# Projections of an attention layer taken two tiles at a time, as seven block products in place of eight

## The chip, the cores and the metric

The kernel runs on one core of a Trainium2 chip. The metric is the device time of one launch in microseconds (us). The kernel before took 3641.48 us, the median of three runs (3638.69 to 3645.62).

The core has five engines with instruction streams of their own: TensorE (PE in the profile, with its weight loads as PEld), VectorE (DVE), ScalarE (ACT), GpSimd (POOL) and SyncE (SP), which here only issues transfers. Each takes its instructions in order and waits on semaphores for the others.

## The reference, cut to what matters

The input x has 64 sequences of 32 tokens of width 512, float32 throughout. Four layers are added to x one after the other. Layer 0 is a linear layer per sequence with a feed-forward part and a normalisation. Layer 1 is a gated feed-forward layer with low-rank updates per sequence. Layer 2 is paged attention, followed by a linear layer with low-rank experts. Layer 3 mixes the tokens of each sequence and applies another linear layer. The change is in layer 2's attention, and in what layer 1 prepares for it:

```python
q = jnp.einsum('bsd,ed->bse', x, Wq).reshape(bsz, seqlen, HQ, D)   # HQ 32, D 128
k = jnp.einsum('bsd,ed->bse', x, Wk).reshape(bsz, seqlen, HK, D)   # HK 8
v = jnp.einsum('bsd,ed->bse', x, Wv).reshape(bsz, seqlen, HK, D)
q = _rope(_rmsnorm(q, q_norm_w), pos)
k = _rope(_rmsnorm(k, k_norm_w), pos)
...                                # 512 cached keys and values per sequence, then the own 32
probs = jax.nn.softmax(scores, axis=-1)
o = jnp.einsum('bhqk,bkhd->bqhd', probs, v_all)
return jnp.einsum('bse,de->bsd', o, Wo)
```

## The kernel before

The 2048 tokens are 16 tiles of 128 tokens, that is of four sequences. The kernel has one stage per layer; in time, layer 0 ends near 390 us, layer 1 near 1059, attention near 3477, and the tail (the rest of layer 2, and layer 3) takes the remainder. The order of the work on TensorE is the order in which the program emits it, since every matmul goes through `c.on_pe` (L74), which chains it to the one before.

**Layer 1** (loop from L512) works through eight groups of two tiles. TensorE computes the gate and up features, `new.features(0)` to `features(10)`. Between those calls stand the calls that load the next group's x and low-rank matrices, and `sum_up` (L272): for each of 16 blocks of Wo, SP loads a row of blocks (`rows`), GpSimd makes four differences of them (`add`, 128x256 each, L289 to L292) and SP stores them to a DRAM buffer `wo_sums` (`store`).

**Attention** is done in two halves, each with four of the eight key heads and half of the query heads, and within a half tile by tile: 32 steps, each with a half h and a tile T. A step has 16 turns, one per sequence and key head, and a turn has two slots, so that two steps, a pair, have 64 slots. Per turn i TensorE transposes the probabilities of turn i (L684), does what is planned for the turn's first slot, takes the scores of turn i+2 (L900), does what is planned for its second slot, and multiplies the values of turn i (L689). The chain of a softmax is scores in PSUM (one buffer), VectorE's multiply by scale with mask and minimum (L905), ScalarE's exponential (L907), VectorE's reciprocal (L909) and product (L912), transposes and ScalarE's copy (L918). At the start of every slot, `slot` (L1044) pops up to two entries of the list `later`: a quarter of the next sequence's key loads (16 transfers of 64 KB make a block of a sequence, from SP) or a load of a piece of Wo (`next_wo`). Cached values are gathered by GpSimd (L715).

The **projections** of a step (class `Projection`, L751) are planned into the slots of the step before, by the tables `plan` (products) and `then` (transposes), L1063 to L1094. For v, k and four groups of query heads, `product` makes an output of 128x512 from four chunks of x, two in each of two slots, into one of two PSUM buffers of the tag "mm" (L786), which the output products also use. A v output is copied by ScalarE. For k and q, `rotated` (L735) runs at once: ScalarE squares the output (L728), VectorE sums the squares (L730), VectorE and GpSimd make the inverse root (L731, L128), VectorE multiplies by cosine and, in two halves, by sine, all read from PSUM (L741, L744), and GpSimd adds the two and multiplies by the root (L747, L748). `turned` (L797) then transposes the result on TensorE. The prologue ahead of the first slot projects the first tile this way. All projection weights of a half, six of 1 MB (`weights`, L953), stay in SBUF; they are loaded at the start and once more at the change of halves.

The **output** of a pair (class `Outputs`, L828) is done in the following pair, by the slots in `ats` (L1109). It is already one of seven block products: the two tiles' output makes a 2x2 block matrix, and so do the weights, some of them the sums made in layer 1. Pieces of Wo of 512 KB come through four buffers; a product that has used one appends `next_wo`. Two tiles `y` are stored by SP at slot 70, that is slot 6 of the pair after. In the last pair the same places hold `tail.weights` and `tail.fold`, which prepare the tail's weights.

## Time and profile before

| | |
|---|---|
| median of three runs | 3641.48 us |
| profiled execution, its own time | 3648.7 us |
| its span, first to last instruction | 3646.9 us |
| TensorE clock granted, mean | 0.998 |
| TensorE busy | 3589.7 us, 19520 instructions |
| VectorE busy | 1894.8 us |
| ScalarE busy | 1296.2 us |
| GpSimd busy | 1415.8 us |
| DMA | 527 MB, mean 145 GB/s |
| attention prologue | 1059 to 1087.5 us |
| first pair, steady pairs | 136.1 us, 149 to 152 us each |

The profile is one execution. A group line reads: source line, engine, operation, output from inputs by the program's names, shapes, count; then busy us and mean ns of one; then the engine's idle time just before them and what ended most of it. A float32 matmul is two instructions on TensorE. Matmuls overlap, so that a sum of their durations is more than the time they take from TensorE. In a window, numbers stand for busy time per engine.

### The profile page before, as it was taken

What the parts mean: (1) busy time and instruction counts of PE and PEld (TensorE: products, weight loads), DVE (VectorE), ACT (ScalarE), POOL (GpSimd) and SP (SyncE); (2) the same over time, 40 slices, a digit from 0 to 9 for tenths busy, and PEclk for the clock granted to TensorE, in tenths of its full rate; (3) what the DMA queues carried; (4) which work ended last, traced back from release to release, by engine and by line L of the source; (5) the groups of instructions that cost most, each with busy time, mean ns of one, the idle gap of its engine ahead of it and who ended that gap; (6) DMA issues with size and microseconds to landing.
All of it is one profiled execution on the core that took longest, in us unless ns stands there. A gap on an engine that the chain in (4) does not pass through costs nothing.

```text
span 3646.9 us, 60352 instructions
## 1 busy us (share of the span) xinstructions
PE 3589.7 (98%) x19520; PEld 2665.6 (73%) x19520; DVE 1894.8 (52%) x4932; ACT 1296.2 (36%) x3046; POOL 1415.8 (39%) x1407
## 2 busy tenths in 40 slices
PE   8999999999999999999999999999999999999999
PEld 3444788888866777777777877778777788777855
DVE  5453222222236655666666656566666666666533
ACT  1111111111115544444444444444444444444311
POOL 0112430000025544555445454454555544545232
PEclk9999999999999999999999999999999999999999
DMA  5004541111124566555555565555555555556631
GB/s 211 24 27 170 171 152 55 50 45 36 38 93 133 149 186 185 155 171 153 185 183 153 181 219 179 179 151 182 174 181 169 156 186 178 170 175 201 218 97 62
DMA packets 527914, 527.15 MB, mean 145 GB/s; under 512 B 54162, under 2 KB 441234, under 8 KB 527602
## 3 DMA queue, kind: packets, MB, share of 16 engines
q1 hardware_dynamic: 480882, 371.21, 32.9%
q0 software_dynamic: 44416, 147.88, 12.6%
q10 hardware_dynamic: 2304, 4.20, 0.3%
q8 instruction: 159, 2.61, 0.3%
q14 instruction: 153, 1.25, 0.1%
HBM read 493.72 MB, written 29.36 MB: 143 GB/s over the span
## 4 chain that ended last, share of the span: by engine, by line
PE 85%; DVE 8%; ACT 2%; DMA 2%; issue 1%; SPq 1%; DVEq 0%; POOL 0%; another core or an unknown queue 0%; ACTq 0%; POOLq 0%
PE po L689 12%; PE sc L900 11%; PE gate_up L342 10%; PE pq L689 9%; PE py L689 9%; PE prT_ps L684 5%; PE pz L342 5%; PE po L1249 3%; PE ph L124 3%; PE pk L689 3%; PE pv L689 3%; PE pd L249 2%; DVE own_vt L722 2%; PE po L342 2%; DVE pr L905 1%; PE qkT_ps L684 1%
## 5 line engine op out<-in xcount | busy, mean ns | idle before, releaser
L715 POOL DMA_INDIRECT vt<-in_v_rows,v_rows x512 | 499.9, 976 | 594.6 <-PE po L689 484.2
L907 ACT ACTIVATE pr<-pr,low 128x544 f32<-128x544 f32 x512 | 383.5, 749 | 703.5 <-DVE low L905 630.4
L689 PEld LDWEIGHTS po<-prT,vt 128*128 128x128 f32 x4096 | 531.3, 192 | 111.1 <-issue 80.7
L900 PE MATMUL sc<-kt,qT 128*128 128x288 f32 (+1 forms) x2048 | 556.3, 394 | 5.5 <-ACT qT L803 1.7
L689 PE MATMUL po<-prT,vt 128*128 128x128 f32 x4096 | 543.9, 276 | 9.5 <-ACT prT L918 6.3
L905 DVE CUSTOM_DVE_ANT_0 pr<-sc,mask 128x544 f32<-128x544 f32 x512 | 368.8, 720 | 321.8 <-PE sc L900 288.5
L900 PEld LDWEIGHTS sc<-kt,qT 128*128 128x128 f32 x2048 | 370.6, 190 | 156.0 <-issue 62.0
L689 PE MATMUL pq<-wq,xT 128*128 128x512 f32 x1024 | 480.6, 592 | 0.0
L918 ACT COPY prT<-prT_ps 128x512 f32<-128x512 f32 x512 | 295.3, 577 | 202.1 <-PE prT_ps L684 147.6
L912 DVE TENSOR_SCALAR pr<-pr,low 128x512 f32<-128x512 f32 x512 | 341.1, 666 | 15.1
L684 PE MATMUL prT_ps<-ident,pr 128*128 128x128 f32 x2048 | 311.2, 275 | 0.1
L689 PEld LDWEIGHTS pq<-wq,xT 128*128 128x128 f32 x1024 | 185.8, 190 | 132.4 <-issue 125.3
L909 DVE RECIPROCAL low<-low 128x1 f32<-128x1 f32 x512 | 83.5, 163 | 340.8 <-ACT pr L907 305.7
L684 PEld LDWEIGHTS prT_ps<-ident,pr 128*128 128x128 f32 x2048 | 238.1, 142 | 7.9 <-issue 0.3
L689 PE MATMUL py<-wo,oT 128*128 128x256 f32 x1024 | 241.4, 379 | 0.0
L128 POOL TENSOR_TENSOR rs<-rs,minus_half 128x4 f32<-128x4 f32 x160 | 169.2, 1058 | 162.9 <-DVE rs L731 158.1
L910 ACT ACTIVATE own_pr<-pr,low 128x32 f32<-128x32 f32 x512 | 164.0, 320 | 131.0 <-DVE low L909 120.3
L747 POOL TENSOR_TENSOR rot<-rot,swapped 128x512 f32<-128x512 f32 x160 | 205.0, 1281 | 5.1 <-DVE swapped L744 3.9
L689 PEld LDWEIGHTS py<-wo,oT 128*128 128x128 f32 x1024 | 187.6, 190 | 21.9
L722 DVE COPY own_vt<-v 32x128 f32<-32x128 f32 x512 | 173.1, 338 | 38.3 <-PE po L689 13.9
L689 PE MATMUL py<-wo,o_sum 128*128 128x256 f32 x768 | 181.3, 379 | 2.1 <-DMA wo<-wo_sums 1.3
L426 DVE TENSOR_TENSOR sg<-sg,gate_up 128x256 f32<-128x256 f32 (+1 forms) x88 | 37.0, 421 | 276.0 <-ACT sg L425 276.0
(226 smaller groups left out, 5192.9 us busy)
## 6 DMA issues: line engine op xcount, KB each, us to landing
kt<-in_kT SPq DMA_DIRECT2D x2048, 64.0 KB
wo<-wo_sums SPq DMA_DIRECT2D x128, 512.0 KB
wo<-in_WoT SPq DMA_DIRECT2D x96, 512.0 KB
xt<-x SPq DMA_DIRECT2D x48, 256.0 KB
A<-in_A SPq DMA_DIRECT2D x64, 152.0 KB
...
```

The costliest lines, as they stand in the source:

```text
L128: self.nc.gpsimd.tensor_tensor(t, t, self.minus_half[:, :n], ALU.pow)
L342: c.on_pe(nc.tensor.matmul(out, lhsT, rhs, start=start, stop=stop))
L684: c.on_pe(nc.tensor.transpose(pt[:, m, :], piece, c.ident))
L689: c.on_pe(nc.tensor.matmul(out, lhsT, rhs, start=first and i == 0, stop=last and i == len(pairs) - 1))
L715: nc.gpsimd.indirect_dma_start(out=vts[b % 2][:, n, :], out_offset=None, in_=a["v_rows"], in_offset=bass.IndirectOffsetOnAxis(ap=rows[h][: ...
L722: nc.vector.tensor_copy(own_vts[b % 2][g * S:(g + 1) * S, g % 2, :], v[j * S:(j + 1) * S, g * HD:(g + 1) * HD])
L747: nc.gpsimd.tensor_tensor(r, r, tmp, ALU.add)
L900: c.on_pe(nc.tensor.matmul(sc[:, lo + n * PSIZE:lo + m * PSIZE].rearrange("p (n k) -> p n k", k=PSIZE), q, kt[:, n:m, g, :], start=True, s ...
L905: nc.vector.tensor_tensor_reduce(pr[:, :NK], sc[:, lo:lo + NK], masks[h, b], -SCALE, 3.0e38, ALU.add, ALU.min, low[:, 0:1])
L907: nc.scalar.activation(pr[:, :NK], pr[:, :NK], AF.Exp, bias=low[:, 0:1], scale=-1.0, accum_out=low[:, 1:2])
L912: nc.vector.tensor_scalar(pr[:, :L], pr[:, :L], low[:, 2:3], None, ALU.mult)
L918: nc.scalar.copy(prT, pt)
```

## The change

The projections of the two tiles of a pair are made together. For each of three groups (k and v, query groups 0 and 1, query groups 2 and 3) x is a 2x2 block matrix (two tiles by two halves of the 512 inputs) and the weights are another (two halves of the inputs by two outputs of 512 columns). Seven products of blocks are made instead of eight, each over two chunks. Products 1 and 5 are copied out of PSUM by ScalarE; the other five are added by VectorE to a tile in SBUF, and two more additions per group are made from SBUF to SBUF. The sums of x blocks are made by GpSimd (`x_sums`). The rotation reads the finished tile in SBUF, writes in place, and is emitted at the start of the next slot (`soon`, `the_rest`).

The weights come in pieces of 512 KB: plain blocks for products 1, 2 and 3, and sums for 4 to 7. The sums of all weights, 40 block sets in place of 16, are made by GpSimd in layer 1, five per group of tiles, with loads on SP, and stored from GpSimd's own queue. Pieces pass through four buffers "wp" and, for the first pair, also through the four "wo"; every product appends a load (`next_wp`) to `later`. All of a pair's projections stand in the pair before, by one table for both steps; the prologue makes those of the first pair. The output products stand at other slots of the pair, from slot 0 and again from slot 53. The tail's weights use buffers of x, work and weight pools.

```diff
-def sum_up(c, pool, sums, h, k):
...
+def sum_up(c, pool, blocks, dst):
+    nc = c.nc
+    w = []
     def rows():
+        w.append(pool.tile([P, 4, D // 2], F32, name="blocks", bufs=2))
+        for n, block in enumerate(blocks):
+            c.load_by(w[0][:, n, :], block)
     def add():
+        t = pool.tile([P, 4, D // 2], F32, name="sums")
+        (b11, b12, b21, b22), (t1, t2, t3, t4) = ([v[:, n, :] for n in range(4)] for v in (w[0], t))
         nc.gpsimd.tensor_tensor(t1, b12, b11, ALU.subtract)
         nc.gpsimd.tensor_tensor(t3, b22, b12, ALU.subtract)
         nc.gpsimd.tensor_tensor(t2, b22, t1, ALU.subtract)
         nc.gpsimd.tensor_tensor(t4, b21, t2, ALU.subtract)
+        nc.gpsimd.dma_start(dst, t)
+    return rows, add
+def column_blocks(a, h, g):
+    if g == 0:
+        return [a[n][:, h * D:(h + 1) * D] for n in ("WkT", "WvT")]
+    at = (h * HKP + 2 * (g - 1)) * D
+    return [a["WqT"][:, at + n * D:at + (n + 1) * D] for n in range(2)]
+def all_sums(c, pool, sums):
+    a, H = c.a, D // 2
+    for h in range(HALVES):
+        for g in range(GB):
+            left, right = column_blocks(a, h, g)
+            for k in range(KC // 2):
+                for n in range(2):
+                    q = slice(n * H, (n + 1) * H)
+                    yield sum_up(c, pool, [w[(k + KC // 2 * i) * P:(k + KC // 2 * i + 1) * P, q]
+                                           for i in range(2) for w in (left, right)],
+                                 sums["in", h][:, g, :, k, q])
+        for k in range(HQP // 2):
+            rows = [(h * HQP + n * HQP // 2 + k) * HD for n in range(2)]
+            yield sum_up(c, pool, [a["WoT"][at:at + HD, n * H:(n + 1) * H] for at in rows for n in range(2)],
+                         sums["out", h][:, k])
...
             def load_x(self):
-                self.xs = [c.load(xp, "xt", [P, D], x_in(G * self.g + t)) for t in range(G)]
+                self.xs = [xp.tile([P, D], F32, name="xt") for _ in range(G)]
+                for t in range(G):
+                    c.load_by(self.xs[t], x_in(G * self.g + t))
...
+            parts = [f for _ in range(5) for f in next(to_sum)]
+            def features(f):
+                new.features(f)
+                if f < len(parts):
+                    parts[f]()
...
+        def the_rest():
+            for f in soon:
+                f()
+            del soon[:]
         def squares_and_root(src):
             tmp = wk.tile([P, REP, HD], F32, name="squares")
             nc.scalar.activation(tmp, src, AF.Square)
-            rs = qp.tile([P, REP], F32, name="rs")
+            rs = qp.tile([P, REP], F32, name="rs", bufs=4)
...
-        def rotated(psrc, tab):
...
+        def rotated(t, tab):
+            src = t.rearrange("p (h d) -> p h d", d=HD)
             ct, st = tab
             rs = squares_and_root(src)
+            tmp = wk.tile([P, REP, HD], F32, name="swapped", bufs=2)
             for lo, hi in ((0, half), (half, 0)):
                 nc.vector.tensor_tensor(
                     tmp[:, :, lo:lo + half], src[:, :, hi:hi + half],
                     st[:, lo:lo + half].unsqueeze(1).to_broadcast([P, REP, half]), ALU.mult)
+            nc.vector.tensor_tensor(src, src, ct.unsqueeze(1).to_broadcast([P, REP, HD]), ALU.mult)
+            nc.gpsimd.tensor_tensor(src, src, tmp, ALU.add)
+            nc.gpsimd.tensor_tensor(src, src, rs.unsqueeze(2).to_broadcast([P, REP, HD]), ALU.mult)
...
+        K2 = KC // 2
+        def wp_tile(name="wp", tag="wp", **kw):
+            return op.tile([P, K2, D], F32, name=name, tag=tag, bufs=4, **kw)
+        def wp_piece(h, g, m, tag="wp"):
+            w = wp_tile(tag=tag)
+            if m in (1, 2, 3):
+                k, n = {1: (0, 0), 2: (1, 0), 3: (1, 1)}[m]
+                src = column_blocks(a, h, g)[n][k * K2 * P:(k + 1) * K2 * P, :] \
+                    .rearrange("(k p) n -> p k n", p=P)
+            else:
+                src = sums["in", h][:, g, {5: 0, 6: 1, 7: 2, 4: 3}[m]]
+            c.load_by(w, src)
+            return w
...
+        class Projections:
+            ORDER = (1, 2, 5, 6, 3, 7, 4)
...
+            def x(self, i):
+                pt = transposes("tq", "xT_ps", [self.xt[i][:, k * P:(k + 1) * P] for k in range(KC)])
+                if i == 0:
+                    self.xT = xp.tile([P, 2, KC, P], F32, name="xT")
+                nc.scalar.copy(self.xT[:, i], pt)
+            def x_sums(self):
+                (x11, x12), (x21, x22) = self.blocks = [
+                    (self.xT[:, i, :K2, :], self.xT[:, i, K2:, :]) for i in range(2)]
+                t = xp.tile([P, 4, K2, P], F32, name="x_sums")
+                s1, s2, s3, s4 = self.s = [t[:, i] for i in range(4)]
+                nc.gpsimd.tensor_tensor(s1, x21, x22, ALU.add)
+                nc.gpsimd.tensor_tensor(s2, s1, x11, ALU.subtract)
+                nc.gpsimd.tensor_tensor(s3, x11, x21, ALU.subtract)
+                nc.gpsimd.tensor_tensor(s4, x12, s2, ALU.subtract)
+            def place(self, g, i, n):
+                if g == 0 and n == 1:
+                    self.v[i] = qp.tile([P, HKP * HD], F32, name="v", bufs=4)
+                    return self.v[i]
+                self.c[g, i, n] = qp.tile([P, D], F32, name="projected", bufs=6)
+                return self.c[g, i, n]
+            def product(self, g, m):
+                (x11, x12), (_, x22) = self.blocks
+                lhs = {1: x11, 2: x12, 3: self.s[3], 4: x22, 5: self.s[0], 6: self.s[1], 7: self.s[2]}[m]
+                w = wps.pop(0)
+                acc = ps.tile([P, D], F32, tag="mm", bufs=2, name="pq" if g else "pkv")
+                part(acc, [(lhs[:, k, :], w[:, k, :]) for k in range(K2)], True, True)
+                d = self.d = {} if m == 1 else self.d
+                if m in (1, 5):
+                    at = (0, 1) if m == 1 else (1, 1)
+                    d[at] = self.place(g, *at)
+                    nc.scalar.copy(d[at], acc)
                     return
+                if m == 2:
+                    d[0, 0] = self.place(g, 0, 0)
+                elif m == 6:
+                    d[1, 0] = self.place(g, 1, 0)
+                to, other = {2: ((0, 0), (0, 1)), 6: ((1, 0), (0, 1)), 3: ((0, 1), (1, 0)),
+                             7: ((1, 0), (1, 0)), 4: ((1, 0), (1, 0))}[m]
+                nc.vector.tensor_tensor(d[to], acc, d[other], ALU.add)
+                if m == 3:
+                    nc.vector.tensor_tensor(d[0, 1], d[0, 1], d[1, 1], ALU.add)
+                elif m == 7:
+                    to = (1, 1)
+                    nc.vector.tensor_tensor(d[1, 1], d[1, 1], d[1, 0], ALU.add)
+                if m != 6 and not (g == 0 and to[1]):
+                    soon.append(partial(rotated, d[to], self.tabs["q" if g else "k", to[0]]))
+            def turned(self, g, i, n):
+                r = self.c.pop((g, i, n)).rearrange("p (h d) -> p h d", d=HD)
                 pt = transposes("tq", "qkT_ps", [r[:, m, :] for m in range(REP)])
+                if g == 0:
+                    self.kT[i] = qp.tile([P, HKP, P], F32, name="kT_own", bufs=3)
+                    nc.scalar.copy(self.kT[i], pt)
+                    return
+                if i not in self.qT:
+                    self.qT[i] = qp.tile([P, HKP, SEQ, REP, S], F32, name="qT", bufs=3)
+                nc.scalar.copy(self.qT[i][:, 2 * (g - 1) + n].rearrange("p j h s -> p h j s"),
...
         ahead = 4
         def wo_tile():
-            return op.tile([P, QH, H], F32, name="wo", bufs=ahead)
+            return wp_tile("wo", "wo").rearrange("p k (n f) -> p (k n) f", f=H)
...
+        wps, wps_to_come = [], [partial(wp_piece, p.h, g, m, "wo" if p is projections[0] and (7 * g + i) % 8 > 3
+                                        else "wp") for p in projections for g in range(GB)
+                                for i, m in enumerate(p.ORDER)]
+        def next_wp():
+            if wps_to_come:
+                wps.append(wps_to_come.pop(0)())
...
+        def products(n):
+            for i in range(count[0], count[0] + n):
+                p.product(i // 7, p.ORDER[i % 7])
+                the_rest()
+                if i < 3 * 7 - 8 or i >= 3 * 7 - 4:
+                    next_wp()
+            count[0] += n
+        count = [0]
+        products(4)
+        load_keys(0, 0, range(2))
+        products(3)
+        load_keys(0, 0, range(2, 4))
...
         def slot(fs):
             now = later[:]
             del later[:]
+            the_rest()
             for f in now[:2]:
                 f()
...
+            def at(i, *fs):
+                to_come.setdefault(s * 2 * per + i, []).extend(fs)
+            if s % 2 == 0:
                 if s == 0:
-                    plan = (("v", 1, 2), ("k", 4, 6), (0, 8, 10), (1, 13, 16), (2, 17, 20), (3, 22, 25))
-                    then = (12, 16, 20, 25, 29)
-                elif s == 1:
-                    plan = (("k", 1, 3), (0, 5, 8), (1, 10, 12), (2, 16, 17), (3, 19, 21), ("v", 24, 27))
-                    then = (10, 13, 19, 24, 28)
-                elif even:
-                    plan = (("v", 1, 2), ("k", 3, 5), (0, 6, 8), (1, 9, 11), (2, 12, 13), (3, 15, 16))
-                    then = (10, 13, 17, 19, 21)
+                    p = projections[0]
+                    at(2, partial(p.turned, 2, 0, 1), partial(own_keys, 0, 1, p.kT[0]))
+                    at(4, partial(p.turned, 2, 1, 1))
+                    at(5, partial(p.turned, 2, 1, 0))
...
+                    p = projections[n + 1]
+                    if n == 0:
+                        ats = ((8, 10, 12, 14, 16, 17, 19), (22, 24, 27, 29, 32, 33, 35),
+                               (38, 40, 43, 46, 48, 49, 52))
+                        then = ((0, 0, 0, 20), (0, 1, 0, 28), (1, 0, 0, 34), (1, 0, 1, 40), (1, 1, 1, 42),
+                                (1, 1, 0, 44), (2, 0, 0, 51), (2, 0, 1, 56), (2, 1, 1, 58), (2, 1, 0, 60))
+                        xs = (0, 1, 2, 3)
+                    else:
+                        ats = ((16, 17, 20, 22, 24, 26, 28), (32, 33, 35, 36, 38, 40, 41),
+                               (43, 44, 46, 47, 48, 49, 51))
+                        then = ((0, 0, 0, 27), (0, 1, 0, 37), (1, 0, 0, 42), (1, 0, 1, 45), (1, 1, 1, 50),
+                                (1, 1, 0, 52), (2, 0, 0, 53), (2, 0, 1, 57), (2, 1, 1, 59), (2, 1, 0, 60))
+                        xs = (9, 11, 12, 13)
+                    for i, f in zip(xs, (partial(p.x, 0), partial(p.x, 1), p.x_sums, p.tables)):
+                        at(i, f)
+                    for *what, i in then:
+                        at(i, partial(p.turned, *what))
+                    for g in range(GB):
+                        for m, i in zip(p.ORDER, ats[g]):
+                            at(i, partial(p.product, g, m), partial(later.append, next_wp))
+                    if n + 2 < len(projections):
+                        at(54, projections[n + 2].load)
                 else:
...
+                    for i, f in zip((4, 8, 12, 16, 20), tail.weights(xp, wk, op, wp_tile)):
+                        at(i, f)
+                    at(45, tail.scaled)
+                    for m, i in enumerate((47, 50, 53, 57)):
+                        at(i, partial(tail.fold, ps, m))
+                if n:
+                    out = outputs[n - 1]
+                    at(0, partial(out.first_sums, nc.gpsimd))
                     if out.h:
+                        at(14, out.befores)
+                    ats = (1, 3, 6, 9, 12, 15, 17, 20, 24, 28, 32, 35, 39, 43) if last_pair else \
+                        (0, 1, 3, 5, 7, 8, 10, 12, 14, 15, 53, 55, 57, 61)
+                    for i, where in enumerate(ats):
+                        at(where, partial(out.product, i), partial(later.append, next_wo))
                         if i in (5, 7):
                             for u in range(2):
+                                at(where, partial(out.next_sum, 6 if i == 5 else 3, u))
+                    at(60 if last_pair else 70, out.store)
+                else:
+                    for i in (40, 46, 52, 58):
+                        at(i, next_wo)
```

## The prediction

> **What bounds the kernel now.** I read the page's busy shares and slices first, then the chain that ended last, then the list of waits of TensorE, then the groups of instructions that the change touches, and last single stretches of the timeline and ten-microsecond windows of one pair of attention steps. A "pair" is two tiles, 64 slots. Busy times and slices:
>
> ```profile
> PE 3589.7 (98%) x19520; PEld 2665.6 (73%) x19520; DVE 1894.8 (52%) x4932; ACT 1296.2 (36%) x3046; POOL 1415.8 (39%) x1407
> ...
> PE   8999999999999999999999999999999999999999
> ...
> DVE  5453222222236655666666656566666666666533
> ...
> DMA  5004541111124566555555565555555555556631
> ```
>
> TensorE is full in every slice; VectorE stands at 5 or 6 tenths in attention (slices 12 to 37), the DMA engines too. The chain and the list of what TensorE waits for say the same:
>
> ```profile
> PE 85%; DVE 8%; ACT 2%; DMA 2%; issue 1%; SPq 1%; DVEq 0%; POOL 0%; another core or an unknown queue 0%; ACTq 0%; POOLq 0%
> ```
> ```profile
> PE po L689 <- ACT prT L918: 6.3, 8, 1.7
> ...
> PE sc L900 <- ACT qT L803: 1.7, 2, 1.0
> PE sc L900 <- DVE low L905: 1.7, 2, 1.0
> ...
> PE py L689 <- DMA wo<-wo_sums: 1.3, 1, 1.3
> ```
>
> In all of attention TensorE's listed waits make some 20 us, so what leaves TensorE leaves the total, as long as the others keep up. From the starts of the probability transposes (L684), a steady pair takes 149.4 us, the first 136.1 us; the stretch ahead of them (the prologue, from the end of layer 1) 28.5 us. I summed TensorE's work slot by slot from the measured durations: 147.6 us in a steady pair, so 1.8 us of it is loss.
>
> The rows that change, and one whole projection half in the timeline:
>
> ```profile
> L689 PE MATMUL pq<-wq,xT 128*128 128x512 f32 x1024 | 480.6, 592 | 0.0
> L909 DVE RECIPROCAL low<-low 128x1 f32<-128x1 f32 x512 | 83.5, 163 | 340.8 <-ACT pr L907 305.7 <-issue 32.2
> L730 DVE TENSOR_REDUCE rs<-squares 128x4 f32<-128x512 f32 x160 | 109.3, 683 | 128.9 <-ACT squares L728 120.5 <-issue 6.7
> L741 DVE TENSOR_TENSOR rot<-pq,q_cos 128x512 f32<-128x512 f32 x128 | 87.1, 680 | 0.0
> L846 DVE TENSOR_TENSOR o_sum<-o_sum,oT 128x512 f32<-128x512 f32 x32 | 22.7, 710 | 13.5 <-issue 8.8 <-PE py L689 4.8
> ```
> ```profile
> 1098.46 1.88 PE L689 MATMUL pk<-wk,xT 128*128 128x512 f32 x4
> ```
>
> Four instructions last 1.88 us, of which the last one's own latency is 592 ns: one costs (1.88 - 0.592) / 3 = 0.43 us of TensorE. Windows of the pair at 1524 (columns: busy us of PE, PEld, DVE, ACT, POOL, then granted clock, DMA share, GB/s):
>
> ```profile
> 1550.00:1560.00 10.00, 10.00 (x50) 6.79 (x49) 8.65 (x20) 5.06 (x13) 5.53 (x6) 1.00 0.42 123
> 1580.00:1590.00 10.00, 10.00 (x61) 9.01 (x61) 4.64 (x12) 4.20 (x13) 3.88 (x4) 1.00 0.90 300
> 1600.00:1610.00 10.00, 9.79 (x64) 7.70 (x63) 4.69 (x16) 3.41 (x9) 4.87 (x6) 1.00 0.91 303
> ```
>
> VectorE at 8.65 of 10, or the DMA at 0.90, left TensorE at 9.8 to 10.
>
> **The skill.** Perfetto Trace Analysis, section Identifying the Most-Contended Engine, says that matmul busy time is a poor measure because matmuls overlap. The trace agrees: busy time of the pq, pk and pv rows is 721.2 us for 1536 instructions, 0.47 each, where the timeline gives 0.43. VectorE: DVE Perf Modes, section Why PSUM operands drop a tier, with the one on tensor_tensor before it, leaves float32 sums of two tensors at the base rate from either memory; the trace agrees, 680 ns from PSUM (L741) and 710 ns from SBUF (L846). SBUF - State Buffer, section Who interferes with whom, says that a VectorE instruction with two SBUF inputs and a GpSimd one that reads SBUF block each other; the rotation now has such inputs, and no row here separates that from the rest. DMA: Bandwidth & Descriptors, section Specifications, gives about 358 GB/s of HBM per core; the busiest windows here show 337.
>
> **The change, part by part.**
>
> Products. Per pair, two tiles by six outputs by four chunks, 48 matmuls, become 3 groups by 7 products by 2 chunks, 42. Each matmul is two instructions (1024 + 256 + 256 = 1536 in 16 pairs), so 6 x 2 x 16 = 192 go. At 0.428 us: -82.2 us; by busy time 721.2 / 8 = -90.2. I take -82 and keep -90 for the range. The transposes (turned, x) stay as many. By place: a steady pair 147.6 to 142.5, the first 124.6 to 119.9, the last, which has no projections, 161.0 to 138.3 (its predecessor does them), the prologue, which now projects two tiles, 24.5 to 41.7. Sum: -4.7 - 14 x 5.1 - 22.7 + 17.2 = -81.6.
>
> VectorE. 15 adds from PSUM and 6 within SBUF per pair, 128x512 each, 0.68 to 0.71 us: 14.5 us a pair, some 230 in all. The rotation keeps its instructions (683 + 262 + 680 + 2 x 414 ns = 2.45 us, ten a pair), reading SBUF, a slot later. VectorE's durations sum to 101.9 us a pair before, while the windows show 93.6 busy (neighbours overlap, factor 0.92); after 116.1, some 107 of 142.5. Before, it also waits per pair 305.7 / 16 = 19.1 us for the exponential and 120.5 / 16 = 7.5 for the squares; its waits for scores (288.5) are slack. 107 + 26.6 = 133.6, so about 9 us a pair stay free. Densest are slots 40 to 53: VectorE 40.6 us of durations, by 0.92 37.4, TensorE 36.2. Both ends: 1.2 to 4.4 us late there, minus what the one or two turns of lead that scores have (2.4 us) absorb: 0 to 3 us a pair. I take 0.5. What is late next is the multiply-and-minimum L905, behind it the exponential, the probability transposes, and with one scores buffer the next scores.
>
> ScalarE copies 6 products a pair instead of 2 v outputs (585 ns): +37 us in all, at 36% busy: nothing; uncovered, 37. GpSimd's x sums, 4 x 0.72 us a pair (the layer-1 timeline has 0.72 for this size), 46 us in all, come three slots ahead of use, behind value gathers: nothing; uncovered, 46. In exchange a product's PSUM bank is freed by one add (0.7 us) and no longer after square, root and rotation: a gain not above the 1.8 us loss per pair.
>
> Layer 1. The sums grow from 16 blocks to 40: 160 subtractions by 0.72 = 115 us on GpSimd with 40 stores from its own queue, and 160 loads of 128 KB on SP. GpSimd is at 0 to 1 tenths there, the DMA at 1 to 2, TensorE at 10: nothing. Queued behind the sums are GpSimd's gathers of the B matrices and SP's loads of A and x, needed some 50 us later; if one came late once a group, 8 x 2 us = 16.
>
> DMA. 12 loads of 1 MB go, 21 x 16 = 336 of 512 KB (176 MB) come: from 171 to about 254 GB/s in attention, share 0.55 to about 0.8. Each waits, on SP's queue, for the product that frees its buffer, and the key loads of the next sequence (16 issues, 8.9 us) stand in the same queue. The tightest load is issued after slot 43 behind such a block: 8.9 us and 3.5 to 6 us to land against about 14.7 us until slot 48. I take 0.2 us a pair, 2 as the upper end. The first eight wait for layer 1 to release memory, as four of the old loads did.
>
> Output store. It moves behind the next pair's first products: its two buffers are written again right after, so ScalarE's copy waits for a store queued behind loads. About 5 us once (pair 2), then 0 to 1.5 a pair, at most partly seen by TensorE: 0.1 a pair.
>
> Prologue. 41.7 us of TensorE work against 37 to 40 on VectorE: two near equal chains, no attention work to fill. Before 4 us of 28.5 were lost; I take 9: +5, bounds 0 and +12. The tail's weights go into other buffers, loaded earlier, nothing.
>
> Sum: -82 + 5 + 14 x 0.8 = -66. In the profiled execution's own time, 3648.7 (span 3646.9 and 1.8 around it), 3582.7. It lies 7.2 above the median of the runs, so there 3641.5 - 66 = 3575.
>
> **The rivals.**
> B, VectorE binds in the dense slots. For it: 8.65 of 10 already before and 14.5 us more. Against: TensorE was full all the same. At 3 us a pair in all instead of 0.8: 14 x 2.2 = 31 more, 3606.
> C, the weight stream arrives late. For it: key blocks of 8.9 us in the same queue, the old weights came only once a half, and TensorE waits 1.3 us for a wo piece. Against: full TensorE at a DMA share of 0.90. At its upper end, 2 us beside the other 0.6: 14 x 1.8 = 25 more, 3600.
> D, slower: VectorE becomes the bound of the whole pair, since it takes its instructions in order and every add waits for its own product. 107 + 26.6 + 15 adds x 1.2 us = 151.6 us a pair in place of 149.4: 14 x 2.2 = 31, with the prologue (+17.2 + 5) and the two end pairs (-27.4) 3667. It decides from (82 - 5) / 14 = 5.5 us of stall a pair, that is from a pair of 142.5 + 1.8 + 5.5 = 149.8 us, or (149.8 - 133.6) / 15 = 1.1 us an add. Against: an add is queued when its product is, and a VectorE that waits for TensorE is ahead of it.
> E, no change: the work saved is used up by stalls of just that size, or TensorE's instructions stay as many. The latter the counts exclude.
>
> **Numbers.** Chances: forecast 0.62, B 0.20, C 0.08, D 0.07, E 0.03. The forecast's own range is 3556 (-90 instead of -82, and none of the 11 us of new stalls) to 3592 (the prologue at its upper bound, +7, and 0.7 us a pair more). The low end goes down to 3550, with a third of the old 1.8 us per pair given back by the PSUM banks. The high end is B with the prologue at its upper bound (+7) and half of what layer 1 could lose (+8), 3621, taken as 3620. Beyond lie D, E and the edges of the others, some 0.17. Within 0.2% (7 us) a measurement can't tell a change from none. Faster 0.90, same 0.03, slower 0.07.
>
> **What would show it.** Right: pq and pkv rows with 1344 instructions; steady pairs of 143 to 146 us, the last about 22 us shorter; VectorE at about 107 of 143 us a pair; layer 1 unchanged within 5 us. B: TensorE waiting for L905 or for the product adds in slots 40 to 55. C: waits for wp or wo loads. D: pairs above 150 us with VectorE's idle before the adds. Wrong would be a GpSimd and VectorE that slow each other (rotation rows well above 680 and 1281 ns), or a layer 1 delayed by its sums.

## The result and the profile after

The changed kernel takes 3693.71 us, the median of four runs (3689.58 to 3700.09), beside 3642.24 us for the kernel before, also the median of four: a ratio of 1.0143 with the interval 1.0124 to 1.0162, so 1.4% slower. The forecast was 3575 us. The profiled execution of the changed kernel took 3696.49 us, with a span of 3694.6.

The page of the changed kernel, busy shares and slices, where before VectorE had 5s and 6s in attention, and TensorE's row had 9s from the second slice on:

```profile
PE 3552.7 (96%) x19328; PEld 2638.9 (71%) x19328; DVE 2149.5 (58%) x5268; ACT 1326.3 (36%) x3110; POOL 1621.6 (44%) x1607
...
PE   8999999999999998999999999999999999999999
...
DVE  5453222222247775867867768677686776877433
...
DMA  5014543333246777777777877777777777787631
```

The 192 instructions of TensorE are gone (19520 to 19328), and its busy time is 37 us less. Yet the span is 47.7 us longer. By stretches, from the ends of layer 1 and the starts of the probability transposes (L706, before L684), with the forecast's parts beside them:

| stretch | before, us | after, us | difference | forecast |
|---|---|---|---|---|
| to the end of layer 1 | 1059.0 | 1070.4 | +11.4 | 0 |
| prologue | 28.5 | 56.9 | +28.4 | +22.2 |
| first pair | 136.1 | 139.2 | +3.1 | -4.7 |
| next 14 pairs | 2095.6 | 2110.8 | +15.2 | -60.2 |
| last pair and all after it | 327.8 | 317.2 | -10.6 | -22.7 |

The 14 pairs hold 75 of the 113 us by which the forecast missed the profiled span. TensorE's waits in the changed kernel, from the first lines of that list:

```profile
PE po L711 <- ACT prT L996: 45.2, 36, 3.3
PE qkT_ps L706 <- POOL rs L130: 15.1, 12, 1.6
PE sc L978 <- DVE low L983: 12.2, 18, 1.2
...
PE py L711 <- issue: 8.0, 1, 8.0
```

The tile prT holds the transposed probabilities, copied out of PSUM by ScalarE; the waits for rs stand for the end of a rotation on GpSimd. To place them I took, for each turn of a pair, the median time from its first transpose to the next turn's over twelve pairs, and subtracted TensorE's work of that turn. In the kernel before, no turn lost more than 0.7 us. In the changed one the loss stands in two places: 2.6 and 0.8 us in turns 21 and 22, 1.8 and 1.0 us in turns 26 and 27. That is 6.2 us, of which the 0.1 us that every turn loses make 0.4: 5.8 us a pair. (Pair and turn times below are of this sort.)

Two windows of the pair that starts at 2476.8 show it (columns as in the windows before):

```profile
2571.50:2581.50 10.00, 7.86 (x29) 5.18 (x27) 9.54 (x17) 3.54 (x8) 8.21 (x8) 0.83 0.82 281
2599.00:2609.00 10.00, 7.89 (x49) 6.36 (x48) 10.00 (x20) 4.14 (x9) 8.19 (x9) 1.00 0.46 119
```

VectorE is at 9.54 and 10 of 10 us and TensorE below 8; GpSimd is at 8 of 10 in both. The timeline of VectorE in the first of them (start, us, engine, line, operation):

```profile
2570.02 0.43 DVE L771 TENSOR_TENSOR swapped<-projected,q_sin 128x256 f32<-128x256 f32 x1
2570.36 0.16 DVE L987 RECIPROCAL low<-low 128x1 f32<-128x1 f32 x1
2570.43 1.99 DVE L771 TENSOR_TENSOR swapped<-projected,q_sin 128x256 f32<-128x256 f32 x1
2572.35 1.26 DVE L990 TENSOR_SCALAR pr<-pr,low 128x512 f32<-128x512 f32 x1
```

and of GpSimd at the same time:

```profile
2570.86 1.27 POOL L775 TENSOR_TENSOR projected<-projected,swapped 128x512 f32<-128x512 f32 x1
2572.21 1.11 POOL L776 TENSOR_TENSOR projected<-projected,rs 128x512 f32<-128x512 f32 x1
```

The first sine product of this rotation takes 0.43 us. The second, started 0.4 us later, takes 1.99 us, while GpSimd adds in the tile of the rotation before; the scaling of the probabilities, 0.48 us elsewhere in this timeline, takes 1.26 beside GpSimd's multiply. TensorE then waits 2.14 us for prT.

That wait does not run through the softmax's own instructions on VectorE. The probabilities were transposed at 2570.90 to 2571.50; what came late is ScalarE's copy of them:

```profile
2575.56 0.63 ACT L757 ACTIVATE squares<-projected 128x512 f32<-128x512 f32 x1 [4.64 <-DVE projected L863]
2576.10 0.57 ACT L996 COPY prT<-prT_ps 128x512 f32<-128x512 f32 x1
```

In ScalarE's order the squares of a rotation stand ahead of the copy, and they waited 4.64 us for a sum of VectorE. All of the 14 pairs have this wait once, with the same squares in front: 1.2 to 2.2 us each, 28.8 us of the 31.9 that TensorE waits for prT there. So VectorE's delay reaches TensorE through ScalarE's order. A kernel with the copy ahead of the squares was not run.

The groups show the delay in the mean. The sine products of q, before from PSUM (first line) and now from SBUF, with the rows around them:

```profile
L744 DVE TENSOR_TENSOR swapped<-pq,q_sin 128x256 f32<-128x256 f32 x256 | 95.6, 414 | 0.0
L771 DVE TENSOR_TENSOR swapped<-projected,q_sin 128x256 f32<-128x256 f32 x256 | 163.2, 649 | 5.5
L774 DVE TENSOR_TENSOR projected<-projected,q_cos 128x512 f32<-128x512 f32 x128 | 89.9, 703 | 0.0
L863 DVE TENSOR_TENSOR projected<-pq,projected 128x512 f32<-128x512 f32 x160 | 109.3, 683 | 27.0 <-PE pq L711 24.8 <-PE sc L978 1.2 <-issue 0.5
L775 POOL TENSOR_TENSOR projected<-projected,swapped 128x512 f32<-128x512 f32 x160 | 207.2, 1295 | 79.8 <-DVE rs L760 78.9 <-DVE projected L774 0.4
```

The mean hides two cases. Of the 320 sine products of q and k, 84 overlap GpSimd's end of a rotation and last 1139 ns in the mean; the other 236 last 421. The adds from PSUM (L863) cost the 683 ns that were forecast. I call the time "held up" by which the instructions of a group last longer than its tenth percentile, summed over VectorE's instructions in attention. It is 221 us in the kernel before (96 in the scaling of the probabilities, 63 in the copies of own values) and 298 after (73 own values, 66 scaling, 61 sine products).

A second effect came with it. The granted TensorE clock falls to half for 3.41 or 6.83 us at some of TensorE's longer stalls: in seven of the fourteen pairs, twice in layer 1, twice in the prologue and once in the first pair. Half of all such stretches is 8.1 us in the kernel before and 37.7 after. As a loss that is an upper figure, since TensorE stands still for a part of them: of the fourteen pairs, the six with a drop of 3.41 us take 150.7 us in the mean and the seven without one 149.7 (the pair with the 8.0 us stall left aside), so 1.0 us and not 1.7.

Theory 1 (in the texts below also the blocking theory): VectorE's rotation, now with two inputs in SBUF, is held up by GpSimd's reads of SBUF. Theory 2 (the density theory): VectorE has too much to do in a few turns, whoever reads what. By my count of its order the program holds 12.7 us of its work in turns 20 and 21 (undisturbed durations, overlap taken off) for 9.9 us of TensorE's. Rivals of both: the weight stream, of whose loads TensorE waits for one in the 14 pairs, 0.6 us, and moved stores.

### The profile page after: what moved, and what is told of

Read it like the earlier page. It is cut to its first block, busy times and chain, and to the rows that moved or that the text cites. A ratio compares the mean times of both kernels' runs of the same rounds, so it can differ in the third digit from the quotient of the medians.

```text
span 3694.6 us, 61434 instructions
## 1 busy us (share of the span) xinstructions
PE 3552.7 (96%) x19328; PEld 2638.9 (71%) x19328; DVE 2149.5 (58%) x5268; ACT 1326.3 (36%) x3110; POOL 1621.6 (44%) x1607
## 4 chain that ended last, share of the span: by engine, by line
PE 82%; DVE 8%; DMA 3%; issue 2%; ACT 2%; SPq 2%; POOL 0%; DVEq 0%; another core or an unknown queue 0%; ACTq 0%; POOLq 0%
PE po L711 13%; PE sc L978 11%; PE gate_up L365 10%; PE py L711 10%; PE pq L711 7%; PE prT_ps L706 5%; PE pz L365 5%; PE pkv L711 4%; PE po L1343 3%; PE ph L126 3%; PE pd L251 2%; PE po L365 2%; SPq L102 2%; DVE swapped L771 1%; DMA kt<-in_kT 1%
## 5 line engine op out<-in xcount | busy, mean ns | idle before, releaser
L737 POOL DMA_INDIRECT vt<-in_v_rows,v_rows x512 | 513.0, 1002 | 610.6 <-PE po L711 498.3
L711 PE MATMUL po<-prT,vt 128*128 128x128 f32 x4096 | 555.7, 279 | 47.2 <-ACT prT L996 45.2
L983 DVE CUSTOM_DVE_ANT_0 pr<-sc,mask 128x544 f32<-128x544 f32 x512 | 368.4, 720 | 183.5 <-PE sc L978 165.4
L706 PE MATMUL prT_ps<-ident,pr 128*128 128x128 f32 x2048 | 315.0, 277 | 2.4 <-DVE pr L990 2.4
L990 DVE TENSOR_SCALAR pr<-pr,low 128x512 f32<-128x512 f32 x512 | 309.2, 604 | 10.4
L706 PEld LDWEIGHTS prT_ps<-ident,pr 128*128 128x128 f32 x2048 | 241.3, 143 | 10.4 <-issue 2.0
L711 PE MATMUL pq<-wp,x_sums 128*128 128x512 f32 x512 | 240.8, 593 | 2.3 <-DVE projected L863 2.2
L775 POOL TENSOR_TENSOR projected<-projected,swapped 128x512 f32<-128x512 f32 x160 | 207.2, 1295 | 79.8 <-DVE rs L760 78.9
L130 POOL TENSOR_TENSOR rs<-rs,minus_half 128x4 f32<-128x4 f32 x160 | 193.7, 1211 | 60.5 <-DVE low L987 49.8
L744 DVE COPY own_vt<-v 32x128 f32<-32x128 f32 x512 | 183.5, 358 | 34.4 <-issue 12.0
L711 PE MATMUL pq<-wp,xT 128*128 128x512 f32 x384 | 187.4, 612 | 1.2 <-DMA wp<-in_sums 0.6
```

Source lines behind the costliest of these rows:

```text
L130: self.nc.gpsimd.tensor_tensor(t, t, self.minus_half[:, :n], ALU.pow)
L706: c.on_pe(nc.tensor.transpose(pt[:, m, :], piece, c.ident))
L711: c.on_pe(nc.tensor.matmul(out, lhsT, rhs, start=first and i == 0, stop=last and i == len(pairs) - 1))
L737: nc.gpsimd.indirect_dma_start(out=vts[b % 2][:, n, :], out_offset=None, in_=a["v_rows"], in_offset=bass.IndirectOffsetOnAxis(ap=rows[h][: ...
L744: nc.vector.tensor_copy(own_vts[b % 2][g * S:(g + 1) * S, g % 2, :], v[j * S:(j + 1) * S, g * HD:(g + 1) * HD])
L775: nc.gpsimd.tensor_tensor(src, src, tmp, ALU.add)
```

## The experiments

All edits are against the changed kernel unless said otherwise; e4 to e10 and e12 to e14 contain the store moves of e3 (in e4 and e10 the output store stands at slot 60). "Pair" is the sum of the 32 turns' medians over twelve steady pairs, which a clock drop in some of them leaves untouched (149.3 before, 149.7 in the changed kernel), "held up" as above. Each batch ran on its own chip with its own runs of the kernel before (3633.6 us for e1 to e4, 3646.3 for e5 to e8, 3640.1 for e9 to e11, 3634.2 for e12 and e13, 3633.3 for e14). The times of e1, e2, e3, e5, e6, e7 and e13 are single runs; their readings rest on waits and durations within the trace. e1, e2 and e5 leave out a part of the computation, so that their q and k (in e2 also v) are not the right ones.

**e1, fills in place of GpSimd's reads**

```diff
-            nc.gpsimd.tensor_tensor(src, src, tmp, ALU.add)
-            nc.gpsimd.tensor_tensor(src, src, rs.unsqueeze(2).to_broadcast([P, REP, HD]), ALU.mult)
+            nc.gpsimd.memset(src, 0.01)
+            nc.gpsimd.memset(src, 0.01)
```

> GpSimd's add and multiply at the end of a rotation (L775, L776) are replaced by two fills of the same 128x512 tile; GpSimd then reads nothing there, and q and k are wrong. Theory 1, VectorE's rotation blocked by GpSimd reading SBUF: the sine products (L771) fall from 649 ns to below 450, the loss after turn 20 and turn 26 falls from 5.8 us a pair to 1 to 3, a steady pair takes 145 to 147 us in place of 150.2, the whole some 60 us less. Theory 2, VectorE has simply too much in turns 20, 21 and 26 (12.7 us of work against 9.9 of TensorE in turns 20 and 21): a steady pair stays within 1.5 us of 150.2.

Measured: 3591.3 us, pair 144.0, at most 0.2 us lost in any of turns 20 to 27, held up 115 us. The group of the sine products in e1:

```profile
L771 DVE TENSOR_TENSOR swapped<-projected,q_sin 128x256 f32<-128x256 f32 x256 | 104.2, 420 | 1.8
```

The pair is 1.1 us under the forecast's (145.1). The packing of turns 20 and 21 is untouched here: in one pair of e1 VectorE works there from 2495.64 to 2508.44 us, 12.8 us, with no gap over 0.05. So the 12.7 us alone do not stop TensorE. The fills are shorter than what they replace, which e5 mends.

**e2, sums by ScalarE's copies**

```diff
-                nc.vector.tensor_tensor(d[to], acc, d[other], ALU.add)
+                nc.scalar.copy(d[to], acc)
...
-                    nc.vector.tensor_tensor(d[0, 1], d[0, 1], d[1, 1], ALU.add)
...
-                    nc.vector.tensor_tensor(d[1, 1], d[1, 1], d[1, 0], ALU.add)
```

> The 15 adds from PSUM of a pair become copies by ScalarE and the 6 adds within SBUF are left out, so q, k and v are wrong; VectorE loses some 13 us a pair, ScalarE gains 9. Theory 2 (too much VectorE work in a few turns): steady pairs 143.5 to 145.5 us, no clock drops in them, the whole 70 to 100 us less than the changed kernel. Theory 1 (blocked by GpSimd): sine products stay at about 650 ns and pairs stay above 147 us.

Measured: 3644.9 us, pair 147.2. All the new sums are gone from VectorE, and still 1.9 us are lost in turn 22 and 1.5 in turn 26; sine products 607 ns, cosine products 1028 (703), held up 296 us, as before the edit (298). The figures are those of theory 1, narrowly for the pair. Less work helps: the added sums are worth 2.5 us a pair here (149.7 to 147.2), and GpSimd's reads 5.7 (to 144.0). The 2.5 are a lower bound, since the edit gives ScalarE 15 more copies a pair, and 1.2 us of the loss in turn 26 is a wait for ScalarE's copy of qT.

**e3, two stores moved**

```diff
-        nc.gpsimd.dma_start(dst, t)
+        nc.sync.dma_start(dst, t)
...
-                    at(60 if last_pair else 70, out.store)
+                    at(60 if last_pair else 63, out.store)
```

> Two moves of stores. The sums of weights are stored by SP and no longer by GpSimd: if GpSimd's own stores make the two unexplained stalls of TensorE in layer 1 (3.8 and 4.1 us, each with a clock drop), both go and layer 1 ends some 12 us earlier; if it is the bytes as such, it stays within 3 us of before. The output store stands at slot 63 in place of 70: the second steady pair, 158.9 us, becomes 150 (stall of 8.0 us and the 3.4 us of clock lost behind it), the other pairs stay at 150. Together -11 to -24 us; if neither is the cause, 0.

Measured: 3655.6 us, 22 us above the kernel before of its batch where the changed kernel was 51 above. Layer 1 ends at 1059.3 us (1070.4; before 1059.0), with none of its two clock drops. The second steady pair takes 148.2 us in place of 158.9. So both stores cost what was expected. In the changed kernel the two stalls of layer 1 stand amid matmuls that wait for nothing the profile shows:

```profile
PE pz L365 <- issue: 4.3, 2, 3.8
PE low_ps L365 <- issue: 4.1, 1, 4.1
```

At both, the DMA engines are full with a 512 KB store and two gathers of GpSimd's queue, and a 16 KB instruction packet lands in the stall: started 1.4 and 1.9 us after TensorE stopped, 1.06 and 0.97 us long, and TensorE goes on 1.3 and 1.2 us after its end. Stores on GpSimd's queue lengthen these stalls but are not what makes them: e3 still stops at both places, for 1.1 and 1.2 us, and the kernel before at the first, for 1.1 us. In the sixteen traces TensorE stops 26 times for 0.9 us or more in layer 1 (420 to 1050 us), and each time it goes on 1.2 to 1.5 us after the end of an instruction packet. So the traces point to late instructions; no run changed anything about those packets. The pair now stands at 148.9: turns 21, 22, 26 and 27 lose 5.3 us (6.2 in the changed kernel).

**e4, an evener table**

```diff
-                        ats = ((16, 17, 20, 22, 24, 26, 28), (32, 33, 35, 36, 38, 40, 41),
-                               (43, 44, 46, 47, 48, 49, 51))
+                        ats = ((4, 6, 8, 10, 13, 16, 18), (20, 22, 24, 26, 29, 33, 36),
+                               (38, 40, 42, 44, 47, 50, 54))
...
-                        xs = (9, 11, 12, 13)
+                        xs = (0, 1, 2, 3)
...
-                        (0, 1, 3, 5, 7, 8, 10, 12, 14, 15, 53, 55, 57, 61)
+                        (1, 2, 4, 7, 9, 11, 14, 15, 19, 21, 31, 34, 52, 56)
```

> The same work as the changed kernel, with both store moves of e3 and another table for the steady pairs: x at slots 0 to 3, products from slot 4 to 54 with rotations at least two slots apart, output products between them. Theory 2: VectorE's arrears never exceed 1 us by my count, so steady pairs take 143.5 to 146 us, the whole 3585 to 3610 and so faster than the kernel before. Theory 1 (blocking by GpSimd, which is as frequent here): pairs 147 to 149 us, the whole 3630 to 3660. If it is neither (transfers late, clock), pairs stay at 150 and the whole at 3670 or more.

Measured: 3730.5 us, ratio to the kernel before 1.0267 (1.0250 to 1.0284), pair 153.9. The whole lies where the third expectation had it, the pair above all three. The sine products are undisturbed (445 ns), and it is the copies of own values that are held up; the same seven take 4.86 us with GpSimd's tables and rotation beside them, where one lasts 0.22 us alone:

```profile
2291.99 4.86 DVE L744 COPY own_vt<-v 32x128 f32<-32x128 f32 x7
```

Turns 25 and 26 lose 4.5 us; at the start of turn 26 TensorE waits 2.4 us a pair for the scaling behind such a stretch. So what is held up is not bound to the rotation's two inputs: copies and scalings from SBUF to SBUF are held up too. Instructions that read PSUM are not (the adds of L863 above, the sine products of e6 below). Other waits of e4 are for ScalarE, 39.3 us in 28 places for its copy of own probabilities (turns 23 and 31); they were not tried apart.

**e5, fills as long as the reads**

```diff
-            nc.gpsimd.tensor_tensor(src, src, tmp, ALU.add)
-            nc.gpsimd.tensor_tensor(src, src, rs.unsqueeze(2).to_broadcast([P, REP, HD]), ALU.mult)
+            for _ in range(4):
+                nc.gpsimd.memset(src, 0.01)
```

> As e1, but each rotation ends with four fills (4 x 0.55 = 2.2 us, near the 1.29 + 1.10 us of the add and the multiply), and with the store moves of e3; q and k are wrong. e1 also shortened GpSimd's work; this one gives the time back and leaves the reading out. If VectorE is blocked by GpSimd's reads: steady pairs 143.5 to 145.5 us as in e1 (144.0). If it was GpSimd's time that counted: 147 to 149.5 us as in e3 (148.9).

Measured: 3594.5 us, pair 144.6. GpSimd is about as busy as in e3 (1554 us for 1595); TensorE loses 0.9 us in turn 26 and 0.1 each in turns 21 and 22. The sine products:

```profile
L771 DVE TENSOR_TENSOR swapped<-projected,q_sin 128x256 f32<-128x256 f32 x256 | 104.5, 421 | 1.8
```

For them it is the reading and not GpSimd's busy time, and the pair falls with them (148.9 in e3). It is not so for all of VectorE: the scaling has a mean of 570 ns here and 564 in e3, and one that starts beside a fill lasts 580 ns in the mean, where 483 is usual with GpSimd idle. A fill is shorter than an add, so whether reading matters there besides length is not separated.

**e6, the rotation from PSUM again**

```diff
-                nc.vector.tensor_tensor(d[to], acc, d[other], ALU.add)
...
-                    soon.append(partial(rotated, d[to], self.tabs["q" if g else "k", to[0]]))
+                nc.vector.tensor_tensor(out, left, d[other], ALU.add)
+                if out is acc:
+                    soon.append(partial(rotated, acc, d[to], self.tabs["q" if g else "k", to[0]]))
+                    the_rest()
```

> The last sum before a rotation is written back into the product's PSUM bank, and the rotation reads it there, as the kernel before did, at once and not a slot later; the rest as e3. Every multiplication then has one input in SBUF. Blocking theory: sine products at 415 to 430 ns (655 in e3), steady pairs 144 to 146.5 us. Rival: the bank is now held through square and rotation, TensorE waits for it in slots 40 to 52, and pairs stay above 148.

Measured: 3671.7 us, pair 149.5. The sine products are back at 414 ns; 60 of them overlap GpSimd's end of a rotation, and these last 413. But the time held up is no less, 304 us: 114 in the scaling of the probabilities (564 ns a piece in e3, 700 here), 89 in own values. GpSimd now delays other instructions. TensorE waits besides 21.5 us in 31 places for a bank still being rotated. The remedy at the input did not pay, and the rival had part of it.

**e7, copies by ScalarE**

```diff
-            nc.vector.tensor_copy(kts[h, b][:, NPP, :].rearrange("p (g s) -> p g s", g=HKP),
+            nc.scalar.copy(kts[h, b][:, NPP, :].rearrange("p (g s) -> p g s", g=HKP),
...
-                nc.vector.tensor_copy(own_vts[b % 2][g * S:(g + 1) * S, g % 2, :],
+                nc.scalar.copy(own_vts[b % 2][g * S:(g + 1) * S, g % 2, :],
```

> The copies of own values and own keys (L744, L731: 239 us of VectorE in the changed kernel, some 100 of it above the time they take undisturbed) go to ScalarE; the rest as e3, the rotation still from SBUF. If any relief of VectorE of this size helps: 15 us a pair less there, losses after turns 20 and 26 below 2 us, pairs 144 to 146. If it is the rotation alone that is blocked: losses stay at 4 to 5 us, pairs at 148 to 149.

Measured: 3673.1 us, pair 149.8. VectorE has some 15 us a pair less to do (239 us in 16 pairs), and turns 21 and 22 lose 4.2 us, more than in e3 (3.1). A relief that does not lie in turns 20 and 21, where the sine products still meet GpSimd (668 ns), brought nothing here. The copies also load ScalarE, through whose order the loss of turn 21 runs (26.6 us of waits with the squares in front), so e7 does not price VectorE's relief alone.

**e8, both**

```diff
-                nc.vector.tensor_copy(own_vts[b % 2][g * S:(g + 1) * S, g % 2, :],
+                nc.scalar.copy(own_vts[b % 2][g * S:(g + 1) * S, g % 2, :],
...
-                nc.vector.tensor_tensor(d[to], acc, d[other], ALU.add)
+                nc.vector.tensor_tensor(out, left, d[other], ALU.add)
```

and the other lines of e6 and e7.

> e6 and e7 together. Blocking theory: steady pairs 143.5 to 145 us, no clock drop in them, the whole 3560 to 3590 us, faster than both kernels. If something else holds the pairs up (transfers, PSUM banks): 147 or more, and 3620 or more.

Measured: 3640.0 us, ratio 0.9987 (0.9978 to 0.9995), pair 147.6, no clock drop in the pairs. TensorE waits 23.1 us for ScalarE's qT and 17.5 for a PSUM bank. From e3's 148.9 that is a quarter of the way to e1's 144.0, and some 3 us a pair above what I had expected from the blocking theory.

**e9, the end of the rotation without GpSimd**

```diff
-            nc.gpsimd.tensor_tensor(src, src, tmp, ALU.add)
-            nc.gpsimd.tensor_tensor(src, src, rs.unsqueeze(2).to_broadcast([P, REP, HD]), ALU.mult)
+            nc.vector.tensor_tensor(src, src, tmp, ALU.add)
+            for m in range(REP):
+                nc.scalar.activation(src[:, m, :], src[:, m, :], AF.Copy, scale=rs[:, m:m + 1])
```

> As e3, but the end of a rotation leaves GpSimd: VectorE adds (0.69 us, ten a pair, +6.9 us), ScalarE multiplies by the root (four of 128x128 a rotation). GpSimd then reads no large tile in the rotation. Blocking theory: sine products at 415 to 430 ns, VectorE's time in a pair stays near 108 us in spite of the added work, steady pairs 144 to 147 us in place of 148.9, the whole some 2 to 3% under e3, so 0.5 to 2% faster than the kernel before. Density theory: turn 20 now holds 10.1 us of VectorE's work by my count in place of 8.8, losses after turns 20 and 26 grow, pairs 150 to 153 us.

Measured: 3665.8 us, ratio 1.0066 (1.0049 to 1.0083), pair 149.2. The sine products are undisturbed (417 ns), held up are 128 us, and turn 26 loses 0.5 us in place of 1.2. But turns 21 and 22 lose 3.7 and 1.4 us: by my count the adds put 1.3 us more into turn 20, and ScalarE has 40 multiplications more a pair. This goes against theory 1 alone. TensorE's waits for prT again have the squares in front (42.4 us in 13 places). Together with e1 it suggests that VectorE may be in arrears by the 3 us of turns 20 and 21, and that either some 2 us of being held up or 1.3 us of more work is too much.

**e10, the table of e4 without GpSimd's reads**

```diff
-                        xs = (9, 11, 12, 13)
+                        xs = (0, 1, 2, 3)
...
-            nc.gpsimd.tensor_tensor(src, src, tmp, ALU.add)
+            nc.vector.tensor_tensor(src, src, tmp, ALU.add)
```

and the other lines of e4 and e9.

> e4's table and e9's rotation together. In e4 VectorE's time was level and pairs took 153.6 us, with copies of own values lasting 4.9 us in place of 1.6 beside GpSimd's reads. Blocking theory: pairs 144 to 146 us, 8 less than e4. If e4's table loses for another reason (the order of transposes and copies on ScalarE): pairs stay above 150 us.

Measured: 3752.3 us, ratio 1.0305 (1.0288 to 1.0323), pair 156.1. Held up are only 83 us, the least of all, and turn 0 loses 5.2 us, where TensorE waits 41.8 us in 14 places for ScalarE's copy of x (3.7 in e4). So with e4's table the x at the start of a pair stands behind the ScalarE work that e9 added for the last rotation, and the waits for ScalarE in turns 23 and 31 stay. The table loses without GpSimd's reads too, and e4 is no test of theory 2. I did not follow it further.

**e11, one part alone in the kernel before**

```diff
-            src = psrc.rearrange("p (h d) -> p h d", d=HD)
+            r = qp.tile([P, REP, HD], F32, name="rot")
+            nc.scalar.copy(r, psrc.rearrange("p (h d) -> p h d", d=HD))
+            src = r
```

This is against the kernel before, with the cosine product moved behind the sine products.

> The kernel before with one part of the change alone: ScalarE copies the projection out of PSUM (0.58 us) and square and rotation read that copy in SBUF; the number of VectorE's and TensorE's instructions stays. Blocking theory: sine products rise from 414 to 550 ns or more, VectorE gains 3 to 5 us a pair; since its rotations stand farther apart, pairs rise from 149.4 to between 149.6 and 153, the whole by 0 to 1.5%. If blocking is no matter of where the input lies: 414 ns stay.

Measured: 3640.5 us, ratio 1.0001 (0.9992 to 1.0010), pair 148.9; sine products 437 ns. Two inputs in SBUF cost next to nothing where rotations stand apart: only 16 of the 320 sine products overlap GpSimd's end of a rotation, against 84 in the changed kernel, and these 16 last 680 ns. The expected 550 ns did not come. Input place alone is not the cause.

**e12, one rotation to a slot**

```diff
+                        p.later = {(1, 0, 1): 39, (1, 1, 1): 43, (1, 1, 0): 45, (2, 0, 0): 47, (2, 0, 1): 50,
+                                   (2, 1, 1): 53, (2, 1, 0): 56}
+                        for what, i in p.later.items():
+                            at(i, partial(p.rotate, *what))
...
+                with tc.issue_after(last_low[0]):
+                    self.waiting.pop(what)()
```

The edit also moves three transposes of the last group one or two slots later.

> As e3, but seven of the ten rotations of a pair get a slot of their own (39, 43, 45, 47, 50, 53, 56), and their VectorE instructions are held behind the scores' multiply-and-minimum (L983) emitted last, so that the compiler's order can't draw two rotations into one turn; four transposes of the last group stand 1 to 2 slots later. All work and GpSimd's part stay. By my count turn 20 holds 6.1 us of VectorE's work in place of 8.8. If both things are needed, several rotations in one turn and GpSimd's reads among them: losses after turns 20 and 26 fall from 5.2 to 1 us, steady pairs 144 to 145.5 us in place of 148.9, the whole 1.5 to 2.2% faster than the kernel before. If GpSimd's reads cost alone, wherever they stand: pairs 147 to 149.

Measured: 3644.3 us, ratio 1.0031 (1.0019 to 1.0042), pair 148.1. Turns 21 and 22 lose 0.1 us each, and the sine products are nearly undisturbed (432 ns). Now GpSimd's work, spread over more turns, delays the copies of own values and of own keys (109 and 45 us held up; 73 and 31 in e3), and turns 25 to 27 lose 3.3 us. The second expectation, that the reads cost wherever they stand, had the pair right.

**e13, the same without GpSimd's reads**

```diff
+                with tc.issue_after(last_low[0]):
+                    self.waiting.pop(what)()
...
-            nc.gpsimd.tensor_tensor(src, src, tmp, ALU.add)
+            nc.vector.tensor_tensor(src, src, tmp, ALU.add)
```

and the other lines of e9 and e12.

> e12 with the end of the rotation on VectorE and ScalarE as in e9: no reads by GpSimd in the rotation, 6 us more of VectorE's work a pair. If packing was what lost in e9 (5.1 us after turn 20): that loss falls below 1 us and pairs take 144 to 145.5 us. If the sum of VectorE's work counts: 148 to 149.5 as in e9.

Measured: 3607.0 us, pair 145.7, held up 97 us. Turns 21 and 22 lose 0.1 us each, where e9 with the same work of VectorE and ScalarE lost 5.1. So with the reads gone it is the packing into turn 20 that counts, not the sum. The packing sets ScalarE's order as well as VectorE's, and the two are not separated.

**e14, two transposes moved**

```diff
-                                (1, 1, 0, 52), (2, 0, 0, 54), (2, 0, 1, 57), (2, 1, 1, 60), (2, 1, 0, 62))
+                                (1, 1, 0, 52), (2, 0, 0, 53), (2, 0, 1, 57), (2, 1, 1, 60), (2, 1, 0, 61))
```

The diff shown is against e13.

> e13 with two transposes moved away from the slot that follows the transposes of own probabilities: query group 2 of the first tile from slot 54 to 53, the last one from 62 to 61. In e13 TensorE waits 20.6 us in 28 places for ScalarE's copy of own probabilities there (1.0 us after turn 26, 0.5 us in turn 31). Both go: steady pairs 144 to 145 us in place of 145.7, the whole 3580 to 3600 us, 1 to 1.6% faster than the kernel before. If the wait only moves to the next transposes: pairs stay at 145.5 to 146.

Measured: 3602.0 us, the median of five runs, ratio 0.9921 (0.9907 to 0.9934); pair 145.6, no clock drop in any pair. The wait for own probabilities turned into one of the same place for qT:

```profile
PE qkT_ps L706 <- ACT qT L891: 14.2, 29, 1.2
PE py L206 <- DVE w L202: 12.2, 3, 11.6
PE po L711 <- ACT prT L1006: 6.6, 8, 1.3
```

so the edit itself brought nothing that can be told from e13. But this version, the block products with the stores of e3, rotations apart and their end off GpSimd, is 0.8% faster than the kernel before and so faster than both. GpSimd is busy for 1199.5 us in it (1621.6 in the changed kernel).

The main readings side by side:

| kernel | us | pair | turns 21+22 | turns 25 to 27 | sine product, ns | held up, us |
|---|---|---|---|---|---|---|
| before | 3642 | 149.3 | - | - | 414 | 221 |
| changed | 3694 | 149.7 | 3.4 | 2.9 | 649 | 298 |
| e1 fills | 3591 | 144.0 | 0.2 | 0.4 | 420 | 115 |
| e3 stores | 3656 | 148.9 | 3.1 | 2.3 | 655 | 279 |
| e5 long fills | 3594 | 144.6 | 0.2 | 1.1 | 421 | 168 |
| e9 no GpSimd | 3666 | 149.2 | 5.1 | 0.7 | 417 | 128 |
| e12 apart | 3644 | 148.1 | 0.2 | 3.3 | 432 | 272 |
| e13 both | 3607 | 145.7 | 0.2 | 1.2 | 416 | 97 |

## Why the prediction was wrong

**Products.** Right. 192 instructions went, and where GpSimd did not read in the rotation (e1) a pair takes 144.0 us for 142.5 of work, so the 5.1 us a pair are there. The changed kernel does not show them, because turns 21, 22, 26 and 27 lose more.

**VectorE.** Here the forecast failed. Its step read "0 to 3 us a pair. I take 0.5", from an average over slots 40 to 53 and from durations undisturbed by GpSimd (by its own figures, 4.4 late less 2.4 of lead, the upper end is 2.0). Measured is a loss of 5.8 us in turns 21, 22, 26 and 27. Three things were wrong with the step.

First, the average hid turn 20. The compiler's order draws two rotations and by my count three sums into one turn, 8.8 us of VectorE's work for 5.6 of TensorE's. The trace of e1, from 2500.61 us, has two rotations and two sums between one multiply-and-minimum and the next, 6.55 us without a gap. I counted by the tables of slots, not by the order in which VectorE's instructions stand.

Second, the time held up had no price. The prediction itself cited the Trainium skill for it, said that the trace does not separate it, and went on without bounding it. A sine product takes 649 ns in place of 414, and 298 us in all are held up in attention in place of 221. The prediction's own sign of being wrong, rotation rows well above 680 and 1281 ns, did not show in those rows (703 and 1295 ns) but in the sine products.

Third, the path. The prediction had the multiply-and-minimum late next, and behind it the exponential and the transposes. In turn 21 the transposes were on time, and the copy of prT stood on ScalarE behind squares that waited for a sum. The waits for the multiply-and-minimum (`low` of L983) are 9.0 us in the 14 pairs, those for prT 31.9.

Rival B named the place and the engine; its price of 3 us a pair was half of the loss, and it had neither the blocking nor the packing of turn 20.

The kernel before did show the blocking, in the scaling of the probabilities:

```profile
L912 DVE TENSOR_SCALAR pr<-pr,low 128x512 f32<-128x512 f32 x512 | 341.1, 666 | 15.1
```

The mean is 666 ns where the lowest tenth takes 480; 512 of them make 96 us above it. A group whose mean lies 40% over its usual value was the row to bound the cost from.

The Trainium skill, SBUF - State Buffer, section Who interferes with whom, has a VectorE instruction with two SBUF inputs contend with a GpSimd instruction that reads SBUF and not with one that only writes it. The runs agree for the sine products (421 ns in e5, 655 in e3). They also show instructions with one SBUF input held up, the scaling, the copies of own values and the mask; the same section says that copies and scalings can run in a two-port mode, which contends with GpSimd, and in e5 the scaling is slower beside fills too (580 ns for 483).

**The clock.** Not in the forecast at all. Of the fourteen waits for prT in turn 21 (1.2 to 2.2 us) six had a stretch of 3.41 us at half the clock with them, and both stalls of layer 1 and the one of 8.0 us had 6.83. At half of each stretch that is 29.6 us more than before, 13.7 of them in the fourteen pairs; this is the upper figure of above.

**Output store.** "About 5 us once (pair 2)": TensorE waited 8.0 us, and up to 3.4 more went by the clock drop with it. The mechanism was right: in that stall ScalarE's copy of y waits 5.3 us for the store, and with the store moved (e3) the stall is gone.

**Layer 1.** "Nothing" was wrong by 11.4 us: two stalls of 3.8 and 4.1 us and a clock drop with each. With e3 the stalls fall to 1.1 and 1.2 us and the drops are gone. The step had counted when GpSimd, SP and the loads would be done. It did not ask what else is late while stores and gathers fill the DMA engines; the instruction packets are what the traces point to.

**Prologue.** +22.2 forecast, +28.4 measured, 2.3 of it clock. The bounds held (+17 to +29).

**First and last pair.** The first was 7.8 us longer than forecast, up to 2.8 of that by the clock. From the last pair 22.7 us of work went, and the stretch from its start to the end is 10.6 us shorter: its turns of 2.2 us of work take up to 3.9 us (turn 9), with 9.2 us of waits for prT in eight places. In turns so short, less work of TensorE brought little, as the waits for prT took its place. I had taken the work for the time.

**DMA and rival C.** Right to set it low: waits for wp are 0.6 us in the whole changed kernel at 241 GB/s and a share of 0.76. Rival D, VectorE the bound of the whole pair, did not occur either: the pairs (150.8 us in the mean) passed its break-even of 149.8 us, but with VectorE busy for 110 of 150 us and the loss in a few turns.

**The range.** It ended at 3620, and the rivals were priced each alone. The loss in the turns, the clock drops at the stalls, the stores, the prologue and the end pairs add up to 113 us.

What stays open: how much of the pair's loss would go with another order of ScalarE's work alone, why e4's table loses as much as it does, and whether the stalls of layer 1 are late instruction packets.
